# Two more key pieces ahead of the loop, one row-score piece inside it: reordering the start of a software-pipelined attention kernel

## Chip, core and metric

The kernel runs on one core of one Trainium2 chip. The metric is device time in microseconds (us) of the whole program. The five engines of the core run their own queues in order: PE (TensorE, matrix products; its weight loads are shown apart as PEld), DVE (VectorE), ACT (ScalarE), POOL (GpSimd), and SP, which here only issues DMAs.

## What is computed

The reference is a stack of six residual blocks over 32 batches of 64 rows and 256 channels. What matters here is the fourth, a cross attention from these rows to a context of 1601 positions per batch, with 16 heads of 16 channels:

```
q = (query @ Wq.T + bq) split into 16 heads
k = (bank @ Wk.T + bk) split into 16 heads     # bank: 1601 x 256 per batch
v = (bank @ Wv.T + bv) split into 16 heads
attn = softmax(q @ k.T / sqrt(16))
out  = (attn @ v) @ Wo.T + bo
```

Ahead of it stand three blocks on the 64 rows alone, each behind a layer norm (one adds a projected mean of the context, one is a self attention, one a feed-forward with experts); behind it stand a recurrent block and a quantised feed-forward.

## The kernel before, in words

Rows are taken 128 at a time, that is two batches, so there are 16 positions. The context of a position is cut into 13 pieces: for each of two batches and each of two channel halves three pieces of 512 context columns (12 in all), and one piece that holds what is left of all four (65 columns each). 16 times 13 is 208 pieces, and the main loop (`for g in range(NU * NT)`, L1392) takes one piece a step. I call `p` the step's place in its position, 0 to 12 (`pos, p = divmod(g, NU)`).

Five functions work on pieces, each called a fixed number of pieces ahead, so that a step of the loop holds parts of several pieces. In the order in which a step issues them:

- `column_scores(g)` (L831): four small products that write minus the row maxima into PSUM tiles `s` (L845), then the scores (L851), then two exponentials on ACT (`pt`, L857). It takes both tiles of the pool `sc`, which has two.
- `values(g + 4)` (L773): products `vps` (L236), copied out by DVE into `vau` (L787).
- `row_scores(g + 5)` (L792): products `r` (L803) into the same two `sc` tiles, then two DVE reductions over the scores (`mx`, L810). These only find the row maxima. A piece's two reductions must be over before the two tiles can be written again, by the next `column_scores` among others.
- `weighted(g)` (L861): products `o` (L875).
- `keys(g + 6)` (L746): products `kps` and one ACT eviction into `kt` (L770), of which there are seven buffers. In the loop the flag `in_columns` makes `mmq` (L239) split the products into four column groups (L248); ahead of the loop they are whole (L244).

For scores and keys (`scanned`, L722) the remainder piece is the first of a position, `p` = 0; for columns and values (`split`, L713) it is the tenth. So once in a position, the call `keys(g + 6)` meets the remainder piece, whose products are shorter: in step `p` = 7.

Around these, a plan of generators (`planned`, `Steps`) runs the other blocks of neighbouring positions at three points of a step: `run(g, 0)` ahead of the row scores, `run(g, 0.5)` behind them, `run(g, 1)` behind the keys. Which of their steps runs in which `g` is fixed by times written in the plan and does not depend on the five functions.

PE, DVE, ACT and POOL run in the order in which the program issues (`tc.manual_schedule`, L1359). Ahead of the loop stands a prologue: a string of letters (L1374), each a call. `a` is a step of the first position's layers (layer norms `a` to `d`, then the queries `qbd`), `b` a step of the second position's first layer, `s` a step of its context sums (ACT, over tiles `part`), `k0` to `k5` are keys, `v0` to `v2` values, `r` the next row scores, `m` the maxima of the first half (`maxima(0)`, five small DVE instructions), `t` their transposition (`maxima_rows(0)`, PE then a DVE copy `neg`), `w` the late weights' loads.

A layer norm goes through three engines (`moments`, L188): DVE statistics, two POOL instructions for the reciprocal root, a DVE scaling `xn`, and then PE transposes (`tp`).

Of the kernel before, what the change touches and what calls it, by code (L numbers as in the profile page):

```python
# [21 lines left out]
NT = NB * S // P  # L22
# [6 lines left out]
NP = L // PIECE  # L29
# [15 lines left out]
def perceiver_kernel(ctx: ExitStack, tc: tile.TileContext, a: dict, out: bass.AP):  # L45
# [676 lines left out]
    def scanned(g):  # L722

        pos, p = divmod(g, NU)
        return (pos, 4 * pos + (p - 1) // NP, (p - 1) % NP) if p else (pos, None, None)
# [23 lines left out]
    def keys(g):  # L749

        pos, h, k = scanned(g)
        if h is None:
            w = wholes[pos]
            w.kt = big.tile([P, 4, TAIL], F32, tag="ktr", name=f"ktr_{w.ti}", bufs=2)
            o = mm_tile([P, 2, 2 * TAIL], f"kps_{w.ti}")
            for oc in range(2):
                mmq2(o[:, oc, :], lambda c: w_k2[:, c, oc * P:(oc + 1) * P],
                     lambda c: w.rest[:, c].rearrange("p b l -> p (b l)"))
            for oc in range(2):
                nc.scalar.activation(w.kt.rearrange("p (b o) l -> p o b l", o=2)[:, oc],  # L760
                                     o[:, oc, :].rearrange("p (b l) -> p b l", b=2), AF.Identity,
                                     bias=chv[:, oc, BK2:BK2 + 1])
            return
        hf = halves[h]
        kt = big.tile([P, PIECE], F32, tag="kt", name=f"kt_{hf.name}_{k}", bufs=7)
        hf.kt.append(kt)
        o = mm_tile([P, PIECE], f"kps_{hf.name}_{k}")
        cT = ctxs[hf.batch]
        mmq2(o, lambda c: w_k2[:, c, hf.oc * P:(hf.oc + 1) * P], lambda c: cT[:, c, k * PIECE:(k + 1) * PIECE])
        nc.scalar.activation(kt, o, AF.Identity, bias=chv[:, hf.oc, BK2:BK2 + 1])  # L770

    def values(g):

        pos, h, k = split(g)
        v = vau[g % 5]
        o = mm_tile([P, 4, P], f"vps_{g}")
        if h is None:
            kr, rest = TAIL, wholes[pos].rest
            for j in range(4):
                mm2(o[:kr, j, :], lambda c: rest[:, c, j // 2, :], lambda c: w_v2[:, c, j % 2 * P:(j % 2 + 1) * P])  # L780
        else:
            kr, hf = P, halves[h]
            cT = ctxs[hf.batch]
            for j in range(4):
                k0 = k * PIECE + j * P
                mm2(o[:, j, :], lambda c: cT[:, c, k0:k0 + P], lambda c: w_v2[:, c, hf.oc * P:(hf.oc + 1) * P])
        nc.vector.tensor_copy(  # L787
            v[:kr, :, 0:VW - 16].rearrange("p k (h d) -> p k h d", d=17)[:, :, :, 0:16],
            o[:kr].rearrange("p k (h d) -> p k h d", d=16))

    def row_scores(g):


        pos, h, k = scanned(g)
        w, qbd = wholes[pos], queries[pos]
        if h is None:
            w.mx = small.tile([P, 4, 4, NP + 1], F32, tag="mx1", name=f"mx1_{w.ti}", bufs=2)
        ps = [sc_tile(f"r_{g}_{m}") for m in range(2)]
        for q in range(4) if h is None else [h % 4]:
            for i in range(4):  # L800
                r = slice(32 * i, 32 * i + 32)
                o = ps[i // 2][:, i % 2, :] if h is not None else ps[i // 2][:, i % 2, q * TAIL:(q + 1) * TAIL]
                nc.tensor.matmul(o, lhsT=qbd[r, q % 2, q // 2].rearrange("p h q -> p (h q)"),  # L803
                                 rhs=w.kt[r, q, :] if h is None else halves[h].kt[k][r, :], start=True, stop=True)
        for m in range(2):
            if h is None:
                nc.vector.tensor_reduce(w.mx[:, 2 * m:2 * m + 2, :, NP],
                                        ps[m][:, :, :4 * TAIL].rearrange("p i (q l) -> p i q l", q=4), AX.X, ALU.max)
            else:
                nc.vector.tensor_reduce(w.mx[:, 2 * m:2 * m + 2, h % 4, k], ps[m], AX.X, ALU.max)  # L810

    def maxima(h):

        hf = halves[h]
        ng = small.tile([P, 4], F32, tag="ng", name=f"ng_{hf.name}")
        nc.vector.tensor_reduce(ng, wholes[hf.pos].mx[:, :, h % 4, :], AX.X, ALU.max, negate=True)
        m = mxp[h % 2]
        nc.vector.tensor_copy(m[:, :, 0], ng)
        nc.vector.tensor_tensor(ng, ng, m[:, :, 0], ALU.subtract)
        nc.vector.tensor_copy(m[:, :, 1], ng)  # L820
        nc.vector.tensor_tensor(m[:, :, 2], ng, m[:, :, 1], ALU.subtract)
# [120 lines left out]
    def projected(pos):  # L942

        w = wholes[pos]
        o = mm_tile([P, D], f"wo1_{w.ti}")
        mmq2(o, lambda c: w.oT[:, c].rearrange("p b s -> p (b s)"), lambda c: w_o2[:, c, :])
        x = work.tile([P, D], F32, tag="x4", name=f"x4_{w.ti}", bufs=1)
        nc.vector.tensor_tensor(x, o, residues[pos], ALU.add)
        return x
# [409 lines left out]
    with tc.manual_schedule(engines={ET.PE, ET.DVE, ET.Activation, ET.Pool}):  # L1359
        ahead, beside, summing = Steps(first()), Steps(first_layer(1, 1)), Steps(early_sums())  # L1360

        def besides():
            if 1 in csums:
                beside.step()

        def scored():
            row_scores(scores.pop(0))

        scores = list(range(5))
        do = {"a": ahead.step, "b": besides, "s": summing.step, "r": scored, "w": late_weights, "m": lambda: maxima(0),  # L1370
              "t": lambda: maxima_rows(0)}
        do |= {f"k{g}": lambda g=g: keys(g) for g in range(6)} | {f"v{g}": lambda g=g: values(g) for g in range(3)}

        for what in """a a a a k1 a a k2 a a s s k3 k0 a a a a s s s s a k4 a v0 v1 a a a s s s s s s b a b a b a b a s w  # L1374
                    a s s a a a b a a s s s r b r b s s s r k5 b r m s s s r v2 t""".split():
            do[what]()
        if beside.gen is not None:
            plan.insert(0, Steps(beside.gen, 0, 4, 28 - beside.done, 2))
        planned(biased(), 3, 5, 2, 1)
        if summing.gen is not None:  # L1380
            plan.insert(0, Steps(summing.gen, 0, 4.5, 37 - summing.done, 0))
        planned(all_ternary(), 5, 23, 24, 2)

        def run(t, place):
            for s in [s for s in plan if s.t0 <= t]:
                s.run(t, place)
                if t >= s.t1 and t < NU * NT - 1:
                    s.all()
                if s.gen is None:
                    plan.remove(s)  # L1390

        for g in range(NU * NT):  # L1392
            pos, p = divmod(g, NU)
            if pos + 1 < NT:
                if p == 0:
                    wholes[pos + 1].rest = load_rest(order[pos + 1])
                if p in (2, 9):
                    load_batch(2 * pos + 2 + p // 8)
            column_scores(g)
            if g == 0:  # L1400
                values(3)
            if g + 4 < NU * NT:
                values(g + 4)
            if p == 1 and pos:
                normalise(pos - 1)
            if g == NU * NT - 2:
                normalise(pos, 3)
            if g + 4 < NU * NT and scanned(g + 4)[2] == NP - 1:
                maxima_rows(scanned(g + 4)[1])
            run(g, 0)  # L1410
            if g + 5 < NU * NT:
                row_scores(g + 5)
                if scanned(g + 5)[2] == NP - 1:
                    maxima(scanned(g + 5)[1])
            run(g, 0.5)
            weighted(g)
            if p == NU - 1 and pos < NT - 1:
                gathered(pos)
            if p == 3 * NP and pos == NT - 1:
                gathered(pos, 3)  # L1420
            if g == NU * NT - 5:
                picked()
            in_columns[0] = True
            if g + 6 < NU * NT:
                keys(g + 6)
            if p == 1 and pos:
                x4[pos - 1] = projected(pos - 1)
            run(g, 1)
            in_columns[0] = False
        normalise_last(NT - 1)  # L1430
        x4[NT - 1] = projected(NT - 1)
        plan.append(Steps(second_layer(NT - 1)))
        while plan:
            for s in list(plan):
                s.step()
                if s.gen is None:
                    plan.remove(s)
# [46 lines left out]
```

## Time and profile before

| what | value |
|---|---|
| median of 3 runs | 2059.86 us (2058.57 to 2060.37) |
| the profiled execution: time | 2059.22 us |
| the profiled execution: span on the core | 2057.5 us |
| PE busy | 1960.1 us, 95% of the span |
| DVE busy | 1300.4 us, 63% |
| ACT busy | 903.7 us, 44% |
| POOL busy | 324.8 us, 16% |
| start of the loop (first L845 product) | 75.27 us |
| mean granted PE clock | 0.982 |

The span is the time from the first to the last instruction; the 1.72 us beyond it lie outside. Busy times of PE are modelled, so a busy PE isn't PE at its peak. The slices of the profile have PE at 5 and 8 tenths in the first two slices (of 51.4 us each), at 9 or more in nearly all others, and at 7 and 5 in the last two.

### The profile page before, as it was taken

To read this page: it belongs to the slowest core of one execution; us is meant where nothing else is said; L and a number is where in the kernel's file an instruction comes from. 1 tells how busy PE (TensorE), PEld (TensorE's weight loads), DVE (VectorE), ACT (ScalarE), POOL (GpSimd) and SP (SyncE) were. 2 spreads that over 40 slices of the span, in tenths; PEclk is the share of its full clock that TensorE was granted. 3 is DMA by queue.
4 is the path that set the end of the run, shared out by engine and by line. 5 is a ranking of instruction groups with operands and counts; after the bars stand their busy time and mean duration, and the time that the engine had idled before them with its cause. 6 is when DMAs were issued, how large, how long until landed. Compare 5 with 4: busy or idle time off the path is not lost.

```text
span 2057.5 us, 79682 instructions
## 1 busy us (share of the span) xinstructions
PE 1960.1 (95%) x36771; PEld 1367.5 (66%) x36771; DVE 1300.4 (63%) x2618; ACT 903.7 (44%) x1402; POOL 324.8 (16%) x543
## 2 busy tenths in 40 slices
PE   5889999999999999999999999999999999999975
PEld 3566677667676766676766676766766666666653
DVE  4556766666666765666667666666667766665654
ACT  4345454454545444444545434343443434334331
POOL 2121111111111111111111111111110111000011
PEclk9899999999999999999999999999999999999996
DMA  9225323221222212112120111111011211101000
GB/s 310 105 90 173 122 85 111 79 89 42 93 90 88 95 36 66 59 58 77 61 76 10 50 40 37 49 40 45 6 58 46 68 45 37 58 2 47 3 12 5
DMA packets 54806, 136.90 MB, mean 67 GB/s; under 512 B 13318, under 2 KB 35016, under 8 KB 54472
## 3 DMA queue, kind: packets, MB, share of 16 engines
q1 hardware_dynamic: 53912, 130.99, 18.8%
q8 instruction: 288, 4.72, 1.0%
q10 hardware_dynamic: 560, 0.81, 0.1%
q14 instruction: 46, 0.38, 0.1%
HBM read 125.53 MB, written 6.25 MB: 64 GB/s over the span
## 4 chain that ended last, share of the span: by engine, by line
PE 87%; DVE 7%; ACT 2%; issue 2%; DMA 1%; POOL 1%; SPq 0%; DVEq 0%; ACTq 0%; POOLq 0%
PE vps L236 18%; PE kps L248 15%; PE r L803 11%; PE o L875 9%; PE s L851 9%; PE ff L236 4%; PE s L845 3%; DVE mx L810 2%; PE ffo L248 2%; PE q L236 1%; ACT pt L857 1%; PE wo L248 1%; PE hg L1004 1%; PE k L236 1%; PE sv L236 1%
## 5 line engine op out<-in xcount | busy, mean ns | idle before, releaser
L857 ACT ACTIVATE pt<-s 128x1024 f32<-128x1024 f32 (+1 forms) x416 | 403.1, 1021 | 265.7 <-PE s L851 265.5
L810 DVE TENSOR_REDUCE mx<-r 128x2 f32<-128x1024 f32 x384 | 451.9, 1219 | 97.4 <-PE r L803 97.2
L236 PE MATMUL vps<-w_L_xattn_WvT,ctxT 128*128 128x128 f32 x3072 | 393.4, 281 | 0.0
L770 ACT ACTIVATE kt<-kps,chv 128x512 f32<-128x512 f32 x192 | 132.0, 687 | 584.9 <-PE kps L248 567.7
L236 PEld LDWEIGHTS vps<-w_L_xattn_WvT,ctxT 128*128 128x128 f32 x3072 | 357.4, 191 | 24.7 <-issue 3.4
L248 PE MATMUL kps<-ctxT,w_L_xattn_WkT 128*32 128x512 f32 x2992 | 356.7, 594 | 0.0
L787 DVE COPY vau<-vps 128x512 f32<-128x512 f32 (+1 forms) x208 | 143.5, 690 | 322.1 <-PE vps L236 320.8
L875 PEld LDWEIGHTS o<-pt,vau 128*32 128x32 f32 (+1 forms) x13312 | 197.7, 110 | 132.2 <-issue 118.5
L875 PE MATMUL o<-pt,vau 128*32 128x64 f32 (+1 forms) x13312 | 230.0, 221 | 5.2 <-ACT pt L857 5.0
L803 PE MATMUL r<-kt,qbd 32*128 32x512 f32 x1536 | 228.9, 647 | 2.8 <-DVE mx L810 2.0
L851 PE MATMUL s<-qbd,kt 32*128 32x128 f32 x6144 | 208.5, 271 | 0.0
L851 PEld LDWEIGHTS s<-qbd,kt 32*128 32x128 f32 x6144 | 205.9, 187 | 3.1
L248 PEld LDWEIGHTS kps<-ctxT,w_L_xattn_WkT 128*32 128x32 f32 x2992 | 83.6, 110 | 112.7 <-issue 112.7
L803 PEld LDWEIGHTS r<-kt,qbd 32*128 32x128 f32 x1536 | 65.9, 184 | 41.0 <-issue 21.2
L845 PEld LDWEIGHTS <-onesb 3*128 3x128 bf16 x768 | 21.3, 91 | 104.2 <-issue 102.1
L845 PE MATMUL s<-neg,onesb 3*128 3x512 bf16 x768 | 82.7, 385 | 5.9 <-DVE mx L810 4.9
L294 ACT ACTIVATE part<-part 128x1601 f32<-128x1601 f32 x48 | 74.1, 1544 | 0.0
L236 PE MATMUL ff<-nT,w_fg 128*128 128x128 f32 x384 | 51.7, 287 | 1.0 <-ACT nT L1039 1.0
L370 POOL TENSOR_TENSOR kbd<-kT,mask 128x512 f32<-128x512 f32 x32 | 32.6, 1040 | 114.9 <-ACT kT L363 114.9
L236 PE MATMUL ff<-nT,w_fv 128*128 128x128 f32 x384 | 50.4, 283 | 0.0
L236 PEld LDWEIGHTS ff<-nT,w_fg 128*128 128x128 f32 x384 | 47.8, 200 | 1.9 <-ACT nT L1039 1.8
L236 PEld LDWEIGHTS ff<-nT,w_fv 128*128 128x128 f32 x384 | 47.9, 201 | 0.0
(384 smaller groups left out, 2376.9 us busy)
## 6 DMA issues: line engine op xcount, KB each, us to landing
ctxT<-ctxT SPq DMA_DIRECT2D x31, 1601.0 KB
part<-ctxT SPq DMA_DIRECT2D x60, 800.5 KB
od<-osb SPq DMA_DIRECT2D x15, 256.0 KB
rest<-ctxT SPq DMA_DIRECT2D x32, 65.0 KB
x<-x SPq DMA_DIRECT2D x16, 128.0 KB
out<-x SPq DMA_DIRECT2D x16, 128.0 KB
w<-w SPq DMA_DIRECT2D x16, 128.0 KB
rs<-od SPq DMA_DIRECT2D x30, 64.0 KB
```

Source lines behind the costliest of these rows:

```text
L236: nc.tensor.matmul(o, lhsT=lhsT(c), rhs=rhs(c), start=(c == 0), stop=(c == 1))
L248: nc.tensor.matmul(o[r], lhsT=lhsT[:, r], rhs=rhs, start=start, stop=stop)
L294: nc.scalar.activation(parts[j], parts[j], AF.Copy, accum_out=csum[:, c, 2 * i + b:2 * i + b + 1])
L370: nc.gpsimd.tensor_tensor(kbd[oc], kT[:, oc, :].rearrange("p (b k) -> p b k", b=2).unsqueeze(2).to_broadcast([P, 2, 4, S]), mask4.unsqueez ...
L770: nc.scalar.activation(kt, o, AF.Identity, bias=chv[:, hf.oc, BK2:BK2 + 1])
L787: nc.vector.tensor_copy(v[:kr, :, 0:VW - 16].rearrange("p k (h d) -> p k h d", d=17)[:, :, :, 0:16], o[:kr].rearrange("p k (h d) -> p k h ...
L803: nc.tensor.matmul(o, lhsT=qbd[r, q % 2, q // 2].rearrange("p h q -> p (h q)"), rhs=w.kt[r, q, :] if h is None else halves[h].kt[k][r, :], ...
L810: nc.vector.tensor_reduce(w.mx[:, 2 * m:2 * m + 2, h % 4, k], ps[m], AX.X, ALU.max)
L845: nc.tensor.matmul(o, lhsT=onesb[r, :], rhs=halves[h].neg[r, :].unsqueeze(1).to_broadcast([3, 4, P]), start=True, stop=False)
L851: nc.tensor.matmul(ps[i // 2][:kr, i % 2, j * P:(j + 1) * P], lhsT=w.kt[r, j, :] if h is None else halves[h].kt[k][r, j * P:(j + 1) * P], ...
L857: nc.scalar.activation(pt[:kr].rearrange("p i k c -> p i (k c)"), ps[m][:kr], AF.Exp)
L875: nc.tensor.matmul(w.o[32 * c:32 * c + 32, q, m, :], lhsT=v[:kr, j, 17 * hd:17 * hd + 32], rhs=pts[m][:kr, c // 2, j, c % 2 * S:c % 2 * S ...
```

## The change

In the prologue's string `k5` moves from behind the row scores to the first wait for a layer norm that has no product beside it (ahead of `tp_c`), and a new `k6` goes into the next (ahead of `tp_d`). The fifth `r` leaves the string. In the loop, step 0 makes up for that: at the place of its row scores it does the fifth piece's (`scored()`), and the sixth piece's come behind its keys (`scan(5)`). From step 1 on, row scores are five pieces ahead, as before. The loop's keys are now seven pieces ahead instead of six.

```
-            do |= {f"k{g}": ... for g in range(6)} | ...
+            do |= {f"k{g}": ... for g in range(7)} | ...
-  ... s s s s s s b a b a b a b a s w
-  a s s a a a b a a s s s r b r b s s s r k5 b r m s s s r v2 t
+  ... s s s s s s b a k5 b a b a b a s w
+  a s s a k6 a a b a a s s s r b r b s s s r b r m s s s v2 t
+        def scan(g):
+            row_scores(g)
+            if scanned(g)[2] == NP - 1:
+                maxima(scanned(g)[1])
...
             run(g, 0)
-            if g + 5 < NU * NT:
-                row_scores(g + 5)
-                if scanned(g + 5)[2] == NP - 1:
-                    maxima(scanned(g + 5)[1])
+            if g == 0:
+                scored()
+            elif g + 5 < NU * NT:
+                scan(g + 5)
             run(g, 0.5)
             weighted(g)
...
             in_columns[0] = True
-            if g + 6 < NU * NT:
-                keys(g + 6)
+            if g + 7 < NU * NT:
+                keys(g + 7)
             if p == 1 and pos:
                 x4[pos - 1] = projected(pos - 1)
+            if g == 0:
+                scan(5)
             run(g, 1)
```

No instruction is added or removed on any engine, except that the moved key piece is issued whole rather than in column groups.

## The prediction

> **What bounds the kernel.** I read the page's busy shares first (PE 95%), then the waits (in the loop PE waits for nearly nothing: its `s` products for DVE `mx` 4.9 us in all 208 steps), then the start in order of time, then the same stretch cut where the granted clock changes. From about 220 us to 1950 us PE is the bound. The first 75 us are a chain through all engines, and there PE also runs at half its clock:
>
> ```profile
> 39.39:42.80 3.41, 0.41 (x2) 0.20 (x2) 1.45 (x4) 2.48 (x5) 0.79 (x2) 1.00 0.90 306
> 42.80:46.21 3.41, 3.25 (x15) 3.25 (x16) 0.42 (x1) 1.24 (x3) 0.00 (x0) 0.50 0.94 283
> 46.21:49.63 3.42, 1.79 (x11) 1.27 (x10) 1.78 (x5) 0.77 (x2) 0.00 (x0) 1.00 1.03 332
> 49.63:53.04 3.41, 1.21 (x4) 0.84 (x5) 0.59 (x2) 0.98 (x2) 0.79 (x2) 0.50 0.53 212
> 63.28:66.69 3.41, 3.41 (x9) 1.18 (x4) 2.56 (x3) 0.00 (x0) 0.00 (x0) 0.50 0.11 38
> 66.69:70.11 3.42, 2.11 (x12) 0.60 (x11) 1.28 (x2) 2.48 (x4) 0.00 (x0) 1.00 0.01 2
> ```
>
> Columns: stretch, length, busy PE, PEld, DVE, ACT, POOL, then the clock. The clock changes only at multiples of 3.41 us on one grid. I cut the whole span on this grid: after a stretch with PE busy up to 0.52 of it the next runs at 0.50, after 0.55 or more it stays (one stretch at 0.74 excepted); from 0.50 it rises only after a stretch busy 0.95 or more (0.87 did not do).
>
> ```profile
> 42.09 0.41 PE L220 MATMUL tp_c<-ident,xn_c 128*128 128x128 f32 x2 [2.77 <-DVE xn_c L202]
> 51.37 0.66 PE L220 MATMUL tp_d<-ident,xn_d 128*128 128x128 f32 x2 [2.69 <-DVE xn_d L202]
> 52.49 2.07 PE L236 MATMUL q<-xT_d,w_L_xattn_WqT 128*128 128x128 f32 x8 [0.46 <-ACT xT_d L226]
> 64.41 3.10 PE L244 MATMUL kps<-ctxT,w_L_xattn_WkT 128*128 128x512 f32 x4
> 75.27 0.40 PE L845 MATMUL s<-neg,onesb 3*128 3x512 bf16 x4 [0.86 <-DVE neg L828]
> ```
>
> The first two are the layer-norm waits that get keys; the fourth is `k5` between the row scores, at half clock.
>
> **1. The prologue, -10.0 us.** A key piece at full clock takes 1.88 (at 20.41). `k5` fills 39.33 to 41.2, `tp_c` starts at 42.09 as before, ACT evicts at 41.6 to 42.3, ahead of the copy at 42.54. The stretch is then busy 0.67 and the clock stays. So `su` and `sv` go as the like pair `k`, `q` at 24.55 (ACT starts 1.25 after, both done after 2.06): `th` 44.21, DVE's three on `m` end at 45.92, `so` starts at 46.03 instead of 47.57. `k6` then takes 47.13 to 49.05. `tp_d`, 3.80 after `so` as before, is at 49.83, so `k6` is out of its way, its eviction too.
> From `tp_d` to the first reduction took 5.74; at full clock 0.47 + 0.42 (copy, then `q`, from 23.65) + 1.22 (`q`) + 1.60 (`qbd`, remainder scores) = 3.7: 53.54 instead of 57.11.
> The reductions then took 57.11, 59.99, 63.40, 68.83. DVE waited for `r` before each (1.02, 0.73, 2.88). At full clock an `r` tile takes 1.1 and DVE is the limit: 53.54 + 1.31 + 0.62 (statistics) = 55.47; + 2.36 + 0.40 (`xn_a`) = 58.23; + 2.36 + 0.28 (`mT`) = 60.87, against 68.83: -8.0. `m` ends 3.40 later as before, at 64.27. The fifth piece's 2.35 of DVE is no longer behind it, so `vau` 0.68 and `neg` follow and the loop starts 0.27 after `neg`: 65.24 instead of 75.27. DVE is late there, not PE: counted by these times, the emptiest stretch of 3.41 (from about 51.0) is 0.58 busy, which is near the bound of 0.53 to 0.55.
>
> **2. Step 0 of the loop, +4.0 us, and its clock, +1.7.** The order of DVE's instructions in the changed kernel is `mx` of the fifth piece, `mx` of the sixth, then `xn_b`, for which `tp_b` waits on PE, and with it `k`, `q` and the next column scores.
>
> ```profile
> 83.18 2.34 DVE L810 TENSOR_REDUCE mx<-r 128x2 f32<-128x1024 f32 x2
> 85.43 0.41 DVE L202 TENSOR_SCALAR xn_b<-x,mv_b,rstd_b 128x256 f32<-128x256 f32 x1
> 83.97 1.90 PE L248 MATMUL kps<-ctxT,w_L_xattn_WkT 128*32 128x512 f32 x16
> 85.98 0.41 PE L220 MATMUL tp_b<-ident,xn_b 128*128 128x128 f32 x2
> ```
>
> On these times the sixth piece's `r` starts when the keys end, 85.87; its reductions start 1.2 later (81.98 to 83.18) at 87.1 and end at 89.45; `xn_b`, then `tp_b` at 90.0 instead of 85.98: +4.0. Of this 1.14 is `r` (work that the prologue lost) and 2.9 is PE standing still, 3.5 with the wait for the copy of `tp_b`. No phase of the grid spreads 3.5 us so that both stretches stay above 0.53 busy, so the clock falls for one full stretch of busy PE: half of 3.41, 1.7; up to 3.1 where the fall comes inside the wait and two stretches go. Bounds 0 and 3.1.
> The Trainium skill ("TensorE: Matmul & The Clock Gate", Part 1) has the clock fall after an idle window of about 3.4 us, free-running. By that this wait, shorter than a window, would mostly cost no clock and the sum would be 1.7 us lower. Our row speaks against it: 39.39 to 42.80 still holds 0.41 of work, and the clock fell.
>
> **3. The loop, +5.4 us.** The remainder's short keys move from step `p` = 7 to `p` = 6. They free 0.95: keys to the next product are 1.84 (511.34 to 513.18) against 0.89 (519.23 to 520.12). In `p` = 7, `pw` (0.98) stands behind them in 14 of 15 positions. In `p` = 6 nothing stands behind the keys in 10, by the order of instructions. So there the next column scores come 2.93 after `r` instead of 3.88. One row shows what that does, a step without keys:
>
> ```profile
> 1946.07 1.20 PE L803 MATMUL r<-kt,qbd 32*128 32x512 f32 x8
> 1948.12 1.90 PE L248 MATMUL kps<-ctxT,w_L_xattn_WkT 128*32 128x512 f32 x16
> 1949.95 0.40 PE L845 MATMUL s<-neg,onesb 3*128 3x512 bf16 x4
> 1951.17 2.05 PE L236 MATMUL vps<-w_L_xattn_WvT,ctxT 128*128 128x128 f32 x16
> 1954.02 1.14 PE L803 MATMUL r<-kt,qbd 32*128 32x512 f32 x8
> 1956.98 0.39 PE L845 MATMUL s<-neg,onesb 3*128 3x512 bf16 x2
> 1957.60 0.39 PE L845 MATMUL s<-neg,onesb 3*128 3x512 bf16 x2 [0.23 <-DVE mx L810]
> 1958.81 1.38 PE L236 MATMUL vps<-w_L_xattn_WvT,ctxT 128*128 128x128 f32 x10
> ```
>
> From `r` to the next `vps` 5.10 with keys, 4.79 with 0.92 less of work: the second `s` tile waits for the reduction, 3.58 after `r`. So `p` = 6 gives back 0.3 of 0.95, while `p` = 7 gets the full 0.95, as PE is the bound there: +0.65 in each of 8 positions (g = 19, 45, 58, 71, 110, 136, 149, 188), 0.2 at g = 84, where other work stands in between: +5.4. Bounds: 0, if the wait is made up later, and 9 times 0.95 = 8.6. At g = 7 PE already waited 0.9 for late reductions, so the longer keys there are free and g = 6 gains 0.3. **The end, -0.3:** step 201 loses its keys, but as above only 0.3 of them counts.
>
> **4. At nothing.** Key buffers: at most six of seven live, the reused one was last read a step earlier. Contexts: needed a step sooner, but they are issued some five steps ahead (92.22 for step 7, which runs at 155.6). SP's order is unchanged and its loads wait for the same instructions; in the prologue ACT reads each `part` at most 1.7 us sooner than now. If a context came late, keys would wait whole microseconds on PE; no such wait is in the list now.
>
> **Sum.** -10.0 + 4.0 + 1.7 + 5.4 - 0.3 - 0.3 = +0.5 on the profiled execution's 2059.22, so 2059.7. The median of the runs is 0.64 above that execution; on that scale **2060.4 us**, no change: 0.2% (4.1 us) is about what a measurement of this kernel can tell.
>
> **Rivals.**
> (a) Slower, 2064.8 (0.17): the clock falls in the row-score chain in spite of the keys, at about 53, because a stretch there is under 0.53 busy. Then `r` goes at the old pace of 3.41 a piece: the three reductions start 1.25, 1.9 and 2.7 late, and `vps` at half clock, 3.9 instead of 2.05, ends behind `m`: the loop starts 4.4 later. For it: 0.58 is near. Against: `r` tiles overlap little at full clock, and each counts 1.1.
> (b) Faster, 2055.0 (0.18): the light steps cost nothing, the sum without 5.4. For it: other queues may catch up in `p` = 7. Against: PE is busy in all of 240 to 360.
> (c) The clock does not fall in step 0: 2058.7 (0.10), no change.
> (d) The change doesn't do what it says, a key piece misses its wait: in 49.05 to 49.83 `k6` has 0.8 to spare; at half clock it would take 3.75 (as at 11.6) and push `tp_d` by 1.05. It is in (a).
> The forecast holds 0.55, 2058.6 to 2062.5 by itself. Range: 2054.5 takes in (b), 2065.0 takes in (a). Chances: faster 0.18, same 0.65 (forecast and c), slower 0.17.
>
> **What would show it.** First L845 at 65.2, no half clock from 39 to 65, `su` to `sv` in 2.1. `xn_b` behind four `mx`, `tp_b` 14.7 after the loop's start instead of 10.7, with a stretch of half clock there. New waits of L845 for DVE `mx` at the eight `p` = 6 steps, about 0.2 us each by the list. If keys or values wait for DMA, or the loop starts after 69, I am wrong.

## The result, and the profile after

The changed kernel takes **2064.24 us** (median of 17 runs, 2059.89 to 2068.99) against 2059.86 for the kernel before on the same chip (17 runs, 2052.53 to 2063.35): ratio 1.0024, 95% interval 1.0014 to 1.0033. It is slower by 4.4 us, just over the bound of 0.2%. The forecast was 2060.4, no change; the time measured is that of rival (a), 2064.8. The profiled execution of after (2068.99, span 2067.3) is the longest of its 17 runs, so I compare stretches of it and not its total.

The start, on the grid on which the clock changes. This is the view by stretches of the changed kernel: stretch, length, busy PE, PEld, DVE, ACT, POOL, then the clock:

```profile
37.95:41.36 3.41, 3.41 (x22) 2.36 (x23) 0.77 (x2) 2.98 (x5) 0.00 (x0) 0.50 0.88 326
41.36:44.78 3.42, 2.43 (x11) 1.16 (x11) 0.68 (x3) 1.60 (x4) 0.79 (x2) 1.00 1.01 290
48.19:51.60 3.41, 2.28 (x7) 0.73 (x5) 1.45 (x4) 0.89 (x2) 0.79 (x2) 1.00 0.90 297
55.02:58.43 3.41, 2.08 (x10) 0.90 (x12) 3.30 (x6) 0.05 (x1) 1.48 (x3) 1.00 1.00 338
58.43:61.84 3.41, 3.41 (x11) 0.79 (x7) 2.78 (x4) 0.00 (x0) 0.00 (x0) 0.50 0.48 185
61.84:65.25 3.41, 3.41 (x12) 1.63 (x12) 2.21 (x4) 1.90 (x3) 0.00 (x0) 0.50 0.16 34
65.25:68.67 3.42, 3.26 (x16) 2.99 (x16) 2.16 (x7) 0.00 (x0) 0.00 (x0) 0.50 0.56 208
```

The same in PE's order of time:

```profile
40.24 2.45 PE L244 MATMUL kps<-ctxT,w_L_xattn_WkT 128*128 128x512 f32 x4
43.22 0.41 PE L220 MATMUL tp_c<-ident,xn_c 128*128 128x128 f32 x2 [0.53 <-DVE xn_c L202]
...
48.15 1.88 PE L244 MATMUL kps<-ctxT,w_L_xattn_WkT 128*128 128x512 f32 x4
50.92 0.44 PE L220 MATMUL tp_d<-ident,xn_d 128*128 128x128 f32 x2 [0.89 <-DVE xn_d L202]
...
58.08 3.21 PE L803 MATMUL r<-kt,qbd 32*128 32x512 f32 x8 [0.72 <-DVE mx L810]
...
64.62 3.78 PE L236 MATMUL vps<-w_L_xattn_WvT,ctxT 128*128 128x128 f32 x16
...
69.32 0.40 PE L845 MATMUL s<-neg,onesb 3*128 3x512 bf16 x4 [0.81 <-DVE neg L828]
```

The two layer-norm waits shrink from 2.77 and 2.69 to 0.53 and 0.89 and the feed-forward runs at full clock. But the stretch 55.02 to 58.43, busy 0.61, is followed by three at half clock: one piece's row scores take 3.21 (1.14 in step 0, at full clock), `vps` 3.78, and the loop starts at 69.32, which is 5.95 earlier than before instead of 10.0.

Step 0, on DVE and then on PE:

```profile
77.23 2.33 DVE L810 TENSOR_REDUCE mx<-r 128x2 f32<-128x1024 f32 x2
81.03 2.36 DVE L810 TENSOR_REDUCE mx<-r 128x2 f32<-128x1024 f32 x2 [1.46 <-PE r L803]
83.30 0.40 DVE L202 TENSOR_SCALAR xn_b<-x,mv_b,rstd_b 128x256 f32<-128x256 f32 x1
```

```profile
79.85 1.14 PE L803 MATMUL r<-kt,qbd 32*128 32x512 f32 x8
83.76 0.44 PE L220 MATMUL tp_b<-ident,xn_b 128*128 128x128 f32 x2 [2.77 <-DVE xn_b L202]
84.72 1.16 PE L236 MATMUL k<-xT_b,w_L_attn_WkT 128*128 128x128 f32 x8 [0.52 <-ACT xT_b L226]
85.71 1.87 PE L236 MATMUL q<-xT_b,w_L_attn_WqT 128*128 128x128 f32 x8
```

`xn_b` stands behind four reductions, `tp_b` comes 14.44 after the loop's start, and `q` runs at half clock (1.87; it took 1.06 in a kernel below whose step 0 kept the clock). Step 0 takes 18.19 instead of 13.65, step 1 0.77 longer: +5.3.

In the waits of PE two rows grew, the first from 4.9 (11 times), the second from 1.7 (2 times):

```profile
PE s L845 <- DVE mx L810: 6.6, 15, 0.7
...
PE s L851 <- issue: 3.5, 3, 1.5
```

Little of the first row's growth is light steps: two of its 15 waits stand behind them (0.20 and 0.18, after g = 19 and 110); six more are 0.14 or 0.15 each, too short for the list. The rest is in other steps, and e2_swap_light below, without these light steps, has 6.1 in 13. The second row was not in my sum: "issue" is time in which PE waited for nothing that the profile shows. All issue waits over 0.2 us in the loop are 3.2 us before and 5.3 after.

### The profile page after: what moved, and what is told of

Its sections match the earlier page's. It is cut to its first block, busy times and chain, and to the rows that moved or that the text cites. A ratio compares the mean times of both kernels' runs of the same rounds, so it can differ in the third digit from the quotient of the medians.

```text
span 2067.3 us, 79630 instructions
## 1 busy us (share of the span) xinstructions
PE 1967.2 (95%) x36743; PEld 1372.9 (66%) x36759; DVE 1300.6 (63%) x2618; ACT 904.0 (44%) x1402; POOL 325.6 (16%) x543
## 4 chain that ended last, share of the span: by engine, by line
PE 84%; DVE 10%; ACT 3%; issue 2%; DMA 1%; POOL 1%; SPq 0%; DVEq 0%; ACTq 0%; POOLq 0%
PE vps L236 18%; PE kps L248 14%; PE r L803 11%; PE o L875 9%; PE s L851 8%; PE ff L236 4%; DVE mx L810 4%; PE s L845 3%; PE ffo L248 2%; ACT pt L857 1%; PE q L236 1%; PE wo L248 1%; PE hg L1004 1%; PE k L236 1%; PE s L393 1%
## 5 line engine op out<-in xcount | busy, mean ns | idle before, releaser
L845 PE MATMUL s<-neg,onesb 3*128 3x512 bf16 x768 | 87.0, 387 | 8.3 <-DVE mx L810 6.6
L845 PEld LDWEIGHTS <-onesb 3*128 3x128 bf16 x768 | 22.4, 91 | 103.3 <-issue 101.4
L417 POOL TENSOR_TENSOR s<-s,mx 128x1024 f32<-128x1024 f32 x15 | 28.6, 1904 | 114.6 <-DVE mx L401 114.6
```

The costliest lines, as they stand in the source:

```text
L845: nc.tensor.matmul(o, lhsT=onesb[r, :], rhs=halves[h].neg[r, :].unsqueeze(1).to_broadcast([3, 4, P]), start=True, stop=False)
```

## The experiments

Each was timed in five rounds against the kernel before, whose median was 2059.6 to 2060.4 on all the chips. "Start" is the first L845, "step 0" the time from there to the first column-score product of step 1, "issue" the sum of issue waits over 0.2 us between the loop's start and 1990 us. These three come from one profiled execution of each kernel: with one and the same prologue up to the loop, after, e2, e3, e6, e8 and e13 (e6 and e13 with `k6` in smaller products) start anywhere from 68.18 to 69.32. The mean granted clock is the mean over the timed runs.

| kernel | median us (runs) | ratio, 95% | start | step 0 | issue | clock |
|---|---|---|---|---|---|---|
| before | 2060.02 (35) | | 75.27 | 13.65 | 3.2 | 0.9807 |
| after | 2064.24 (17) | 1.0014-1.0033 | 69.32 | 18.19 | 5.3 | 0.9815 |
| e1_scores_back | 2064.51 (12) | 1.0010-1.0031 | 72.77 | 13.65 | 3.6 | 0.9808 |
| e2_swap_light | 2055.87 (11) | 0.9976-0.9998 | 68.96 | 19.01 | 4.0 | 0.9830 |
| e3_six_ahead | 2062.58 (12) | 1.0004-1.0024 | 68.18 | 17.04 | 6.6 | 0.9805 |
| e4_both | 2063.94 (12) | 1.0005-1.0030 | 72.16 | 14.78 | 6.3 | 0.9808 |
| e6_six_cols | 2057.43 (12) | 0.9977-1.0004 | 69.07 | 18.00 | 3.6 | 0.9818 |
| e7_fill | 2055.22 (12) | 0.9973-0.9999 | 66.82 | 18.81 | 4.2 | 0.9843 |
| e8_late_max | 2053.24 (12) | 0.9958-0.9985 | 68.38 | 14.54 | 3.8 | 0.9830 |
| e9_fill_late | 2048.79 (7) | 0.9932-0.9971 | 66.22 | 14.54 | 3.5 | 0.9863 |
| e10_waits_undone | 2072.53 (6) | 1.0041-1.0081 | 75.46 | 19.36 | 3.8 | 0.9782 |
| e11_no_swap | 2060.46 (12) | 0.9996-1.0018 | 68.96 | 16.18 | 4.9 | 0.9839 |
| e12_both_cols | 2056.91 (12) | 0.9971-0.9998 | 71.96 | 13.63 | 3.5 | 0.9822 |
| e13_cols | 2066.87 (12) | 1.0014-1.0042 | 68.94 | 18.69 | 5.0 | 0.9817 |

The last column explains the spread. In the 35 runs of the kernel before, time and clock go together (correlation -0.90, 1.4 us for each 0.001). I use that 1.4 below to say how much of a difference of times is clock; it ties time to clock and proves no cause. Within the changed kernels the rate is 1.1 to 2.4, and the clock column holds the half clock of the start too, so what is put down to clock is rough.

### Keys out of the waits: e10_waits_undone

```diff
- ... b a k5 b a b a b a s w a s s a k6 a a b a a s s s r b r b s s s r b r m s s s v2 t
+ ... b a b a b a b a s w a s s a a a b a a s s s r b r b s s s r k5 b r k6 m s s s v2 t
```

> The changed kernel with one part undone: the sixth and seventh pieces' keys leave the two waits for the layer norms and stand between and behind the last two row scores instead. All else is as changed. Theory (keys in the waits keep the clock up in the feed-forward and the query, and this is worth the 6 us at the start that the change has over the kernel before, together with 2.4 for the fifth piece's reductions): half clock again at 42.5 and 49.5, the first L845 at 74 to 76 instead of 69.3, the time 2064.2 + 5.5 = 2069.5. Rival (the start is bound by VectorE's reductions, and the keys' place counts little): the first L845 at 70 to 71, the time 2065.5.

Measured: start 75.46, 2072.53. In PE's order of time of this kernel the waits and the half clock are back:

```profile
42.42 0.66 PE L220 MATMUL tp_c<-ident,xn_c 128*128 128x128 f32 x2 [2.77 <-DVE xn_c L202]
43.54 2.08 PE L236 MATMUL su<-xT_c,w_L_ffn_sw1T 128*128 128x128 f32 x8 [0.46 <-ACT xT_c L226]
...
53.09 0.66 PE L220 MATMUL tp_d<-ident,xn_d 128*128 128x128 f32 x2 [2.69 <-DVE xn_d L202]
```

`tp_d` at 53.09 instead of 50.92, `su` 2.08 instead of 1.16. The theory holds: keys in the waits bring the loop's start forward by 6.1, and the median says 8.3.

### The light steps: e2_swap_light

```diff
-            if g + 7 < NU * NT:
+            if p == 6 and g + 8 < NU * NT:
+                keys(g + 8)
+            elif p == 7 and g + 6 < NU * NT:
+                keys(g + 6)
+            elif p not in (6, 7) and g + 7 < NU * NT:
                 keys(g + 7)
```

The remainder's short keys are back in `p` = 7, and a whole piece's are in `p` = 6.

> The changed kernel, but the remainder's short keys are called in step p = 7 again and the next position's first keys a step earlier, in p = 6: only the order of two calls in each position. My theory (light steps without anything behind the keys lose 0.52 to 0.65 us each): 5.4 us less than the changed kernel, about 2059 us, and no wait of the column scores for the reductions after p = 6. Rival (the light steps cost nothing, the loss is the start's clock and step 0): no change against the changed kernel, 2064 us.

Measured: 2055.87, 8.4 less than the changed kernel and by the interval faster than the kernel before. Step 45 (`p` = 6) of the changed kernel in order of time, then of e2_swap_light:

```profile
509.69 1.20 PE L803 MATMUL r<-kt,qbd 32*128 32x512 f32 x8
...
511.74 1.07 PE L248 MATMUL kps<-rest,w_L_xattn_WkT 128*32 128x130 f32 x32
512.74 0.92 PE L845 MATMUL s<-neg,onesb 3*128 3x512 bf16 x4
513.28 1.28 PE L851 MATMUL s<-qbd,kt 32*128 32x128 f32 x32
514.49 2.05 PE L236 MATMUL vps<-w_L_xattn_WvT,ctxT 128*128 128x128 f32 x16
```

```profile
509.14 1.20 PE L803 MATMUL r<-kt,qbd 32*128 32x512 f32 x8
...
511.19 1.90 PE L248 MATMUL kps<-ctxT,w_L_xattn_WkT 128*32 128x512 f32 x16
513.02 0.39 PE L845 MATMUL s<-neg,onesb 3*128 3x512 bf16 x4
513.25 1.06 PE L851 MATMUL s<-qbd,kt 32*128 32x128 f32 x32
514.24 2.05 PE L236 MATMUL vps<-w_L_xattn_WvT,ctxT 128*128 128x128 f32 x16
```

From `r` to `vps` it is 4.80 with the short keys and 5.10 with the long ones: 0.3 comes back for 0.83 of keys, as L845 takes 0.92 instead of 0.39, waiting for the reduction of its second tile. Step 46 then has the 0.83 on top. The net price is 0.47 to 0.59 in each of nine positions (my eight and g = 162), 0.14 at g = 84 (read in e1 and e13, which have no issue wait there), -0.3 at the end: **4.6 us** where I had 4.8 with g = 6 and the end. The other 3.8 of the difference are not these steps: 1.3 is issue waits (5.3 to 4.0), and the clock is 0.0015 higher, about 2.1 by the rate above.

### Scores back in the prologue, keys six ahead: e1, e3, e4

```diff
# e1_scores_back
- ... r b r b s s s r b r m s s s v2 t
+ ... r b r b s s s r b r m s s s r v2 t
-            if g == 0:
-                scored()
-            elif g + 5 < NU * NT:
+            if g + 5 < NU * NT:
                 scan(g + 5)
...
-            if g == 0:
-                scan(5)
# e3_six_ahead
-            if g + 7 < NU * NT:
-                keys(g + 7)
+            if 0 < g and g + 6 < NU * NT:
+                keys(g + 6)
```

e4_both has both edits.

> The changed kernel with the fifth row scores back in the prologue and the sixth's at their old place in step 0; the keys stay as changed (k5, k6 in the waits, seven ahead). My theory (the step 0 wait of PE for xn_b behind four reductions, 4.0 us, and a stretch of half clock behind it, 1.7): the loop starts 2.4 later than in the changed kernel, step 0 is back at about 13.6 us, in all 3.3 less: about 2061 us. Rival (step 0 hides the scores, what was lost is the clock in the prologue): only the 2.4 are seen, about 2066.5 us.

> The changed kernel with the loop's keys six ahead as before; step 0 has no keys, since the seventh piece's are done in the prologue. My theory: the light steps are back at p = 7 (5.4 less), step 0 gains at most 0.3, because the sixth piece's scores wait for the fifth's reductions, and the end gives 0.3 back: about 2059 us. Rival (step 0 is bound by PE's work, the light steps cost nothing): only the 1.9 us of keys go from step 0, about 2062.3 us.

> Both of the others: keys in the waits of the prologue, five row scores in the prologue, the loop six ahead with no keys in step 0. My theory: start 7.6 earlier than before the change, step 0 shorter by its keys (1.9), nothing lost in the loop: about 2051 us, faster than the kernel before by 0.4%. Rival (the gain of the start is lost to the clock in the row scores): the start is only 3 earlier, about 2055 us.

Measured: 2064.51, 2062.58 and 2063.94; none came down as the theory had it. e1: with the fifth piece's scores in the prologue the loop starts 3.45 later and steps 0 and 1 are exactly as before, 5.3 shorter. That is a gain of 1.9 by the profiles, which the medians don't show (+0.3). The fall of the clock is the reason that it is not more: in e1 it is down for 13.65 us, from 58.4 on, because a fifth piece runs in it. e3: the light steps are gone as meant, and in their place stand new issue waits. Its time is that of its rival, but not for the rival's reason: the light steps do cost (e2), and step 0 is 1.15 shorter, not 1.9. e4: the loop starts at 72.16, not at the 67.7 expected. The terms don't add up to these medians: by start, steps 0 and 1, light steps and issue, e1, e3 and e4 would lie 3.6, 5.9 and 4.5 below the changed kernel, and they lie 0.3 above, 1.7 and 0.3 below. The clock column accounts for 1.0 to 1.4 of that at the rate above; the rest is open (each interval is some 2 us to either side). One step of e3 in PE's order of time shows the new wait, with the remainder's column scores:

```profile
408.38 0.45 PE L842 MATMUL s<-neg,onesb 3*65 3x128 bf16 x16
408.62 0.49 PE L851 MATMUL s<-qbd,ktr 32*65 32x128 f32 x9
410.22 0.88 PE L851 MATMUL s<-qbd,ktr 32*65 32x128 f32 x23 [1.11 <-issue]
```

Nine of 32 products, then 1.11 us in which nothing is waited for. From step 1 on e3 has the order of instructions of the kernel before, which has no such wait here. What differs is where they lie: with the seventh piece's keys issued whole, 12 products and 12 weight loads fewer come ahead of them.

### Where the instructions lie: e6, e12, e13

```diff
-        do |= {f"k{g}": lambda g=g: keys(g) for g in range(7)} | ...
+        def sixth():
+            in_columns[0] = True
+            keys(6)
+            in_columns[0] = False
+        do |= {f"k{g}": lambda g=g: keys(g) for g in range(6)} | {"k6": sixth} | ...
```

The same work in 16 products instead of 4, in e3 (e6_six_cols), e4 (e12_both_cols) and the changed kernel (e13_cols).

> The loop of e3_six_ahead (keys six pieces ahead, none in step 0), but the seventh piece's keys of the prologue go to TensorE in sixteen column-group matmuls instead of four whole ones, so that as many TensorE instructions lie ahead of the loop as in the kernel before. Theory (the stalls of TensorE marked issue inside the remainder's column scores depend on where these instructions lie in the instruction stream): the sum of issue waits in the loop goes back from 6.8 us to about the 3.2 of the kernel before, and the time from 2062.6 to about 2059. Rival (the stalls come from something else that e3 changed, such as the missing keys in step 0): the sum stays near 6.8 and the time near 2062.6.

> e4_both (row scores of five pieces in the prologue, keys six ahead and none in step 0) with the seventh piece's keys of the prologue in sixteen column-group matmuls. Theory (issue waits move with the place of instructions in the stream): the sum of issue waits in the loop 6.3 to about 3.5, the time 2063.9 - 2.8 = 2061.1 or less; that e6_six_cols was no chance. Rival (the 5 us between e3_six_ahead and e6_six_cols came from where the half-clock stretches fell): the sum still near 6, 2063 to 2064.

> The changed kernel, but the seventh piece's keys of the prologue go to TensorE in sixteen column-group matmuls instead of four whole ones, so that the loop's instructions lie where they lay in the kernel before. Nothing else differs. Theory (a part of the change's loss are issue waits, which move with the place of the instructions): the sum of issue waits in the loop 5.3 to about 3.4, the time 2064.2 - 2 = 2062.2 or less, and the light steps unchanged (p=6 and p=7 together 6 us longer than before). Rival (in the changed kernel the stalls have another cause, since its order of instructions differs from before's anyway): the sum stays at 5 or more, 2064.

Measured: e6 2057.43, e12 2056.91, e13 2066.87. The same step of e6 in PE's order of time:

```profile
410.47 0.45 PE L842 MATMUL s<-neg,onesb 3*65 3x128 bf16 x16
410.72 1.07 PE L851 MATMUL s<-qbd,ktr 32*65 32x128 f32 x32
```

In e6 and e12 the issue waits fall from 6.6 and 6.3 to 3.6 and 3.5, as expected, and the medians by 5.2 and 7.0, more than expected: 3.0 and 2.8 are issue, and the clock is 0.0013 and 0.0014 higher, 1.8 and 2.0. So the same work issued as twelve products more in the prologue takes away stalls 300 us and more later; 3 us of each pair's 5 to 7 are shown to be these. In e13 the theory fell: the stalls only moved (1.38 at 775.4 in place of 0.87 at 873.8, for one), their sum stays at 5.0. e13's median is 2.6 above the changed kernel's with nearly the same start, steps and sum; why is open. So the place of the instructions decides where PE stalls, but matching the count of the kernel before helps only where the order is also that of before.

The traces also say which property of the place it is. Every kernel moves some 288 packets of 16 KB on a queue marked instruction, as after's page has it (queue, packets, MB, share):

```profile
q8 instruction: 288, 4.72, 0.9%
```

That is one for every 256 of PE's some 73,700 recorded products and weight loads. The 14 traces have 59 issue waits over 0.2 us; 14 of them are the same 1.52 us at g = 3. All of the other 45 stand at one place in such blocks of 256 (the 184th to 194th when PE's records are counted, of which some are missing), and each ends 1.2 to 1.6 us after one of these packets landed (in e3 above, 408.86 and 410.22), where 5% of PE's products do. The reading that fits is that PE stands in these waits until its next block of instructions has come: twelve products and twelve weight loads more shift the borders of the blocks by 24, out of some dense stretches of small products and into others. 31 of the 45 lie in steps `p` = 9, where the remainder's small products stand. No run changes this loading itself. Nor is a stall's price its length alone: in after the one of 1.47 that ends at 1263.20 is followed by a stretch of half clock, and step 126 is 2.0 longer than before with 0.4 more of stall. And a wait of 1.35 in e4 at 1011.55, put down to a DVE copy and so not in its 6.3, stands at the same place of a block and is not there in e12.

### The clock in the row-score chain and `xn_b`: e7, e8, e9, e11

```diff
# e7_fill: e2_swap_light and
+        def fill():
+            o = mm_tile([P, PIECE], "fill")
+            nc.tensor.matmul(o, lhsT=w_k2[:, 0, 0:P], rhs=ctxs[0][:, 0, 0:PIECE], start=True, stop=True)
- ... s r b r b s s s r b r m s s s v2 t
+ ... s r f b r f b s s s r f b r m s s s v2 t
# e8_late_max: e2_swap_light and, in step 0, the products of row_scores(5) alone;
# its two tensor_reduce are issued by layer0 right behind xn_b
+        xn = normalised(tile_([P, D], "xn", "xn_b"), m)
+        if hooks:
+            hooks.pop()()
```

e9_fill_late has both on top of e2_swap_light; e11_no_swap has both on the changed kernel.

> The kernel e2_swap_light with three added whole-array matmuls (128x128 by 128x512, 0.94 us each, result read by nobody) in the prologue, one behind each of the first three row scores, in the waits for their reductions. Theory (what is lost at the loop's start against my sum is the clock that falls in the row-score chain): no half clock between 53 and 69 us, the first L845 at 65.5 instead of 68.96, the time 2055.9 - 3.4 = 2052.5. Rival (the clock falls in row-group matmuls however full TensorE is): the loop starts at 69 or up to 1 later, 2056 to 2057.

> The kernel e2_swap_light, but in step 0 the reductions of the sixth piece's row scores go to VectorE behind xn_b instead of ahead of it (their matmuls stay where they are). Theory (step 0 is longer because xn_b stands behind four reductions): tp_b 11.7 instead of 14.4 us or more after the loop's start, step 0 longer than before's by 1 to 2 instead of 5.4, the time 2055.9 - 3.9 = 2052.0. Rival (step 0 is bound by the sum of VectorE's work, so that the reductions only move to the next wait): step 0 and 1 together still 5 longer, 2055.9.

> e7_fill and e8_late_max together. Theory: both gains add, 2055.9 - 3.4 - 3.9 = 2048.6, faster than the kernel before by 11 (ratio 0.9945). Rival (a clock that is kept at the start falls one stretch later in step 0, and takes 1.7 to 3.4 back): 2050.3 to 2052.

> e9_fill_late without the swap of the remainder's keys, which is the changed kernel with the three added matmuls in the row-score chain and with the reductions of step 0 behind xn_b. Theory (the light steps cost what the profiles add up, 6.3 us, of which I had forecast 5.4): 2048.8 + 6.3 = 2055.1. Rival (they cost what the medians of e2_swap_light and the changed kernel differ by, 8.4): 2057.2. The start and step 0 as in e9_fill_late (66.2, 14.5).

e8 in DVE's order of time, and its `tp_b` in PE's:

```profile
76.29 2.34 DVE L821 TENSOR_REDUCE mx<-r 128x2 f32<-128x1024 f32 x2
78.54 0.41 DVE L202 TENSOR_SCALAR xn_b<-x,mv_b,rstd_b 128x256 f32<-128x256 f32 x1
80.09 2.36 DVE L811 TENSOR_REDUCE mx<-r 128x2 f32<-128x1024 f32 x2 [1.14 <-PE r L807]
```

```profile
78.91 1.14 PE L807 MATMUL r<-kt,qbd 32*128 32x512 f32 x8
79.98 0.44 PE L220 MATMUL tp_b<-ident,xn_b 128*128 128x128 f32 x2
```

`tp_b` comes 11.60 after the loop's start (68.38) and waits for nothing; step 0 is 0.9 longer than before, which is about the 1.14 of `r`. The median is 2053.24, 2.6 less than e2_swap_light, where 3.9 was expected. The step-0 term is shown: PE stood still because `xn_b` was queued behind reductions.

e7, the stretches of its row-score chain and the chain itself (L1371 is the added product):

```profile
51.88:55.29 3.41, 2.90 (x42) 2.03 (x40) 1.79 (x6) 2.58 (x3) 0.00 (x0) 1.00 0.49 129
55.29:58.70 3.41, 3.41 (x15) 1.19 (x14) 3.11 (x6) 0.21 (x2) 1.48 (x3) 1.00 1.03 383
58.70:62.11 3.41, 3.41 (x18) 1.43 (x16) 3.19 (x5) 0.52 (x2) 0.00 (x0) 1.00 0.30 104
```

```profile
57.04 1.13 PE L1371 MATMUL fill<-ctxT,w_L_xattn_WkT 128*128 128x512 f32 x2
58.09 2.19 PE L803 MATMUL r<-kt,qbd 32*128 32x512 f32 x8
60.21 1.13 PE L1371 MATMUL fill<-ctxT,w_L_xattn_WkT 128*128 128x512 f32 x2
61.49 1.38 PE L803 MATMUL r<-kt,qbd 32*128 32x512 f32 x8
62.80 2.05 PE L236 MATMUL vps<-w_L_xattn_WvT,ctxT 128*128 128x128 f32 x16
66.82 0.40 PE L845 MATMUL s<-neg,onesb 3*128 3x512 bf16 x4 [0.48 <-DVE neg L828]
```

No stretch of half clock up to the loop, `vps` 2.05 instead of 3.78, and the start at 66.82: work that nobody reads brings the loop 2.1 forward against e2_swap_light (68.96). In e9 it is 66.22. The median of e7 shows little of it (2055.22 against 2055.87), that of e9 against e8 does (2048.79 against 2053.24; clock 0.9863 against 0.9830). Why e7 gains less than e9 from the same edit I can't say; the intervals leave room for either. **e9 is the fastest kernel here**, 0.5% below the kernel before, and its 2048.79 is the 2048.6 expected.

In e11's profiled execution the clock fell all the same, at 53.55, before the first added product (54.75) could count. Its stretches:

```profile
50.13:53.55 3.42, 2.23 (x25) 1.66 (x26) 1.26 (x5) 2.00 (x5) 0.00 (x0) 1.00 0.50 185
53.55:56.96 3.41, 3.41 (x30) 1.79 (x34) 1.85 (x5) 1.59 (x2) 0.18 (x1) 0.50 0.95 281
```

So filling helps where the grid happens to let it. The median of e11 is 2060.46, 11.7 above e9, where 6.3 (theory) and 8.4 (rival) were expected. My 6.3 held an issue wait at g = 84 and was too high for the steps themselves; light steps 4.6, issue 1.4 (4.9 against 3.5) and clock (0.9839 against 0.9863, 3.4, of which a part is the start's, 2.7 later than e9's) make 9.4; the rest is open.

## Why the prediction was right or wrong

**Forecast.** 2060.4, measured 2064.24. The range held it; the sign tipped over the bound. By the prediction's own sign ("or the loop starts after 69") its start was wrong. The terms by the profiles: -6.0 (start), +5.3 (steps 0 and 1), +4.6 (light steps), +2.1 (issue), together +6.0 against my +0.5; the medians say +4.4, within 2.9 to 6.8.

**Step 1, -10.0: failed, measured -6.0.** The parts up to the query went as written: `su` 1.16, `sv` 1.06, `k6` 1.88, no eviction in the way. The sub-step that failed is "the emptiest stretch of 3.41 (from about 51.0) is 0.58 busy, which is near the bound of 0.53 to 0.55", from which I let the clock stay. It fell after 55.02 to 58.43 at 0.61. Its price from `tp_d` to the loop's start is 18.4 instead of 15.4, and in e7 and e9, with the chain filled, 16.2. The remaining 1.1 is an earlier fall (37.95 to 41.36, after a stretch busy 0.53), which no other trace with the keys in the waits has: `k5` took 2.45 and `tp_c` came at 43.22 instead of 42.09. My bound came from stretches without row scores; the one that I excepted (524.08 to 527.49 of before, busy 0.74) holds the remainder's. In stretches with row scores the clock fell at 0.61 (after), 0.65 (e11), 0.66 (e8), 0.67 (e1) and 0.72 (e2), while stretches of products over all 128 rows at 0.56 to 0.63 kept it (e7: 41.63, 48.46, 34.81). No bound on the busy share parts them: with row scores it was kept at 0.73 (51.60 of after), and over 128 rows it fell at 0.62 (1975.24 of e8). At half clock it is alike: 58.43 to 65.25 of after, two stretches full of row scores at busy 1.00, did not bring the clock back, where I had it rise after 0.95. That row scores count for less than the busy time says is an argument from these stretches; no kernel here tests it alone. An estimate from the records of all 14 traces supports it. Let every product count its columns, at the 0.92 ns a column of whole f32 products (1.88 for four of 512) and 0.47 in bf16, times the share of the 128 x 128 array that it uses, rows and columns rounded up to 32. Then the 128 stretches at half clock (from 17 to 1995 us) part cleanly: the 51 that stayed lie at 0.39 or less (58.43 to 65.25 of after at 0.31 and 0.34), the 77 that rose at 0.42 or more, where the best bound on busy share puts 26 wrong. At full clock a bound of 0.40 has 27 of 7981 wrong, the best on busy share 49 (82 fell). Rival (a) had the right mechanism and nearly the start (4.4 later than forecast, so 69.64), but not the place (about 53) nor the bound (under 0.53). That the total came within 0.6 of its 2064.8 is luck in part, as it has no issue waits.

**Step 2, +4.0 and +1.7: right**, +5.3 for the two. `tp_b` 14.44 after the start (14.7 forecast), half clock in one stretch, and e8 takes nearly all of it away by moving two reductions.

**Step 3, +5.4, with g = 6 and the end +4.8: right in its mechanism**, 4.6 by steps, with the 0.3 given back in `p` = 6 and the full price in `p` = 7 as forecast. That the sum fits so well is luck: the keys free 0.83 and not 0.95, so a position costs 0.53 and not 0.65, but there are nine and not eight (g = 162 was missing), and g = 6 gave nothing. The forecast of 5.4 for e2 was low since the clock and the issue waits change as well.

**Step 4, nothing for buffers, contexts and SP: right**; no wait of keys or values for a DMA in the loop is in after's list. **What was missing** is the stalls in issue, +2.1 by the profiles, put at nothing. That no instruction is added and one piece is issued whole looked like nothing, and in e3 and e4 its undoing went with 5 to 7 us.

**The clock's window.** The Trainium skill ("TensorE: Matmul & The Clock Gate", Part 1) has a free-running window of about 3.4 us and says that the same kernel varies from run to run with its phase. The 3.41 us grid and the correlation of -0.90 above agree. Its condition for the fall, an idle window, does not: here the clock fell after windows busy 0.43 (82.34 to 85.75) and 0.61, and the measurement decides.

## What to carry to other kernels

Before work is moved into a wait, ask what the next wait does to the clock: the gain lasts only as far as PE stays full, and here the chain behind took back 3 us of it. An operand that PE waits for belongs ahead of bulk reductions in DVE's order (2.6 us by the medians, 4.5 by the step, for one move). Where the granted clock explains most of the spread, list it for all runs beside the times, and price a step by its own length in the trace, not by a difference of two medians.

## What was not expected of the hardware

- Stalls of 0.2 to 2.0 us in PE's issue, mostly in steps with dense small products, which move when 12 products and their weight loads are added in the prologue: sums of 3.2 to 6.6 us in kernels of nearly the same work. 45 of 45 lie at one place in PE's blocks of 256 instructions.
- Added products that compute nothing made a kernel faster at its start by 2.1 us, as they kept the clock through three stretches.
- The spread of 5 to 15 us between runs of one kernel is the clock to a large part: correlations between time and mean granted clock of -0.68 to -0.97 in the thirteen changed kernels.
